# Both feed-forward matrices by Strassen's algorithm, in groups of four token tiles

## The chip, the cores and the metric

The kernel runs on one core of a Trainium2 chip, as one launch. The core has TensorE (PE, matrix products into PSUM; its weight loads are listed as PEld), VectorE (DVE), ScalarE (ACT), GpSimd (POOL) and SyncE (SP, which here only issues DMAs). Each works through its own list of instructions in order, and waits on semaphores for the others. The metric is device time of the whole launch in microseconds.

## The reference, cut to what matters

All data are float32. `x` has 8 batches of 1024 tokens with 512 features: 64 token tiles of 128.

```python
xn = layernorm(x)                                   # over the 512 features
# attention branch, head size 128
local  = softmax(q k^T / sqrt(128)) v               # local_qkv_w
sparse = softmax(only scores >= the 102nd largest of the row) v   # sparse_qkv_w
mem    = concat(p, softmax(p bank^T) bank) @ mem_out_w + b        # p = xn @ memory_proj_w
pred   = gelu((xn @ pred_in_w + b) @ pred1_w + b) @ pred2_w + b
s = concat(local, sparse, mem, pred) @ warboss_w + warboss_b
# feed-forward branch
g = silu(relu(xn @ w1 + b1) @ w2 + b2)              # w1: 512 x 2048, w2: 2048 x 512
out = x + s * g
```

## The kernel before, in words

Tokens are taken per batch (8 tiles), in pairs of tiles (`T` = 256 tokens) for the projections, heads and feed-forward. Normalized tokens are transposed on TensorE into `xnT` (features on partitions), in tiles of four token tiles. Keys, values and queries come from resident weights `w_qkv`; each token tile then has a local and a sparse score row of 1024. The sparse head finds the 102nd largest score on VectorE with 13 rounds of MAX8 and MATCH_REPLACE8 (`sparse_select`). Probabilities are transposed on TensorE, and `attend` multiplies them by the values per pair.

The feed-forward branch goes by pairs. `up` (lines 412 to 433) computes two of the 16 blocks of 128 hidden columns directly: per block four matmuls (128x128 weights by 256 tokens) accumulate over the four 128-row parts of `w1`, which lies in SBUF whole (lines 211 to 214). ScalarE applies bias and Relu from PSUM; GpSimd makes four sums of the 128x128 quarters (lines 427 to 433). `down` (435 to 451) multiplies by `w2` with Strassen's algorithm in its Winograd form: seven products in place of eight per chunk, accumulated over the eight chunks (`NWC`) of a pair in four PSUM banks (`ps_f`). The sums of `w2`'s quarters are made once, written to DRAM, and loaded per chunk as 896 KB tiles with three buffers (`load_w2`, 352 to 370). `make_gate` (383 to 405) copies the seven sums to SBUF, adds them into four quarters on GpSimd, adds the bias and applies Silu. `finish_pair` (686 to 707) waits for gate and heads, multiplies by `warboss_w`, and GpSimd adds the bias, multiplies by the gate, adds `x` and issues the output DMA.

PSUM has four banks in a ring (`ps_r`) for all products that are copied out at once, and the four of `ps_f`.

The order of the work is written out when the program is built. A planner (lines 108 to 170) keeps a clock per engine, counted in matmul columns. Work around the feed-forward consists of chains (generators), each of which says what it next waits for: a clock time, or facts in the set `done`. `run` advances the first chain that is ready; when none is, it takes the next matmul of the feed-forward branch (`filler`) if `may_fill` allows. Instructions stay in the order in which they are emitted on every engine (`InOrder`). Each token tile starts at `begin + n * STEP` of that clock. Thus feed-forward matmuls fill TensorE wherever attention waits for other engines. A wrong estimate in the planner costs nothing by itself: the chip waits on semaphores alone.

Of the kernel before, what the change touches and what calls it, by code (L numbers as in the profile page):

```python
# [15 lines left out]
P = 128  # L16
# [4 lines left out]
def kernel(  # L21
# [50 lines left out]
    ps_f = ctx.enter_context(tc.tile_pool(name="ps_f", bufs=1, space=PSUM))  # L72
# [36 lines left out]
    SLACK = 400  # L109
    rounds = []  # L110
# [20 lines left out]
    def run(until):  # L131

        while not until():
# [8 lines left out]
            else:  # L142
                columns = next(filler, None) if may_fill() else None
                if columns is not None:
                    tick(columns)
                else:
                    times = [c[0] for c in chains if not callable(c[0])]
                    if not times and not rounds and not any(map(is_ready, chains)):
                        raise RuntimeError("nothing is due")
                    tick(max(1, min(times + [clock["pe"] + 200]) - clock["pe"]))  # L150

    def start(generator, due=0):
        chains.append([due, generator])
# [17 lines left out]

    def ring(name, shape):
        return ps_r.tile(list(shape), F32, tag="r", name=name)
# [5 lines left out]
    def load_x(name, b, j):  # L179
        t = sb.tile([P, D], F32, tag="x", name=f"{name}_{b}_{j}", bufs=4)  # L180
        sp.dma_start(out=t, in_=x[b, ts(j, P), :])
        return t


    first_x = [load_x("xl", 0, j) for j in range(4)]
    w_qkv = const.tile([P, ND, 2, 3 * HD], F32, tag="w_qkv", name="w_qkv")
    for h, w in ((SPARSE, sparse_qkv_w), (LOCAL, local_qkv_w)):
        sp.dma_start(out=w_qkv[:, :, h, :], in_=w.rearrange("(c p) n -> p c n", p=P))
        t = sb.tile([P, 2, D], F32, tag="s", name=f"xl_0_{h}", bufs=2)
        for k in range(2):  # L190
            j = len(first_x)
            sp.dma_start(out=t[:, k], in_=x[0, ts(j, P), :])
            first_x.append(t[:, k])

# [16 lines left out]
    w1 = const.tile([P, ND, W], F32, tag="w1", name="w1")  # L211
    w1v = ffn_w1.rearrange("(c p) n -> p c n", p=P)
    for c in range(4):
        pool.dma_start(out=w1[:, :, ts(c, W // 4)], in_=w1v[:, :, ts(c, W // 4)])
    b2 = const.tile([P, D], F32, tag="b2", name="b2")
    pool.dma_start(out=b2, in_=ffn_b2.partition_broadcast(P))
    w_mp = load_const("w_mp", memory_proj_w)
    w_pi = load_const("w_pi", pred_in_w)
    w_p1 = load_const("w_p1", pred1_w)
    w_p2 = load_const("w_p2", pred2_w)  # L220
    w_wb = load_const("w_wb", warboss_w)
# [77 lines left out]
    def project_k(b, g, h):  # L299
        if b not in kT:  # L300
# [4 lines left out]
            [w_qkv[:, c, h, HD : 2 * HD] for c in range(ND)],  # L305
# [6 lines left out]
    def project_v(b, q):  # L312
# [4 lines left out]
        for j in range(2):  # L317
# [3 lines left out]
                [w_qkv[:, c, :, 2 * HD :] for c in range(ND)],  # L321
# [7 lines left out]
    def project_q(b, p):  # L329
        qT[b, p] = sb.tile([P, 2, T], F32, tag="qT", name=f"qT_{b}_{p}", bufs=2)  # L330
        ps = ring(f"pq_{b}_{p}", (P, 2, T))
        for h in range(2):
            accumulate(
                ps[:, h, :], [w_qkv[:, c, h, :HD] for c in range(ND)], pair_xnT(b, p), T
            )
# [7 lines left out]

    H = D // 2
    B11, B21, T2, T3, T4, T1, B22 = range(7)
    w2_dram = [
        dram.tile([P, 7, H], F32, tag=f"w2_{k}", name=f"w2_{k}_dram") for k in range(NWC)
    ]
    w2_tiles = {}
    w2v = ffn_w2.rearrange("(h k p) n -> p k h n", h=2, p=P)  # L350

    def load_w2(n):

        pair, k = divmod(n, NWC)
        if pair >= B * NP:
            return
        w = sb.tile([P, 7, H], F32, tag="w2", name=f"w2_{n}", bufs=3)
        w2_tiles[n] = w
        if pair:
            sp.dma_start(out=w, in_=w2_dram[k])  # L360
            return
        b12 = sb.tile([P, H], F32, tag="tmp", name=f"b12_{k}", bufs=3)
        sp.dma_start(out=w[:, B11 : B21 + 1, :], in_=w2v[:, k, :, :H])
        sp.dma_start(out=w[:, B22, :], in_=w2v[:, k, 1, H:])
        sp.dma_start(out=b12, in_=w2v[:, k, 0, H:])
        pool.tensor_sub(w[:, T1], b12, w[:, B11])
        pool.tensor_sub(w[:, T2], w[:, B22], w[:, T1])
        pool.tensor_sub(w[:, T3], w[:, B22], b12)
        pool.tensor_sub(w[:, T4], w[:, B21], w[:, T2])
        sp.dma_start(out=w2_dram[k], in_=w)  # L370
# [3 lines left out]


    gate = {}
    at_pair = [0, 0]

    def may_fill():
        b, p = at_pair  # L380
        return b == B or needs("constants", ("xnT", b, 2 * p), ("xnT", b, 2 * p + 1))()

    def make_gate(b, p, acc):
        n = f"{b}_{p}"
        m = sb.tile([P, 7, H], F32, tag="m", name=f"m_{n}")
        for c in range(4):
            w = min(2, 7 - 2 * c)
            copy(m[:, 2 * c : 2 * c + w, :], acc[:, 2 * c : 2 * c + w, :], 180 * w)
        add = pool.tensor_add
        add(m[:, 1:3], m[:, 1:3], twice(m[:, 0]))  # L390
        add(m[:, 3:7:3], m[:, 3:7:3], twice(m[:, 2]))
        add(m[:, 6], m[:, 6], m[:, 5])
        add(m[:, 4:6], m[:, 4:6], twice(m[:, 3]))
        g = sb.tile([P, 2, D], F32, tag="g", name=f"g_{n}")
        for j, blocks in enumerate((m[:, 1:7:5], m[:, 4:6])):
            add(
                g[:, j].rearrange("p (h n) -> p h n", h=2), blocks,
                b2.rearrange("p (h n) -> p h n", h=2),
            )
        on("pool", 1200 + 4500)  # L400
        yield after("pool")
        act.activation(g, g, AF.Silu)
        on("act", 700)
        gate[b, p] = g
        done.add(("gate", b, p))

    def feed_forward():

        hidden = {}
        acc = {}  # L410

        def up(b, p, c):
            at_pair[:] = b, p
            ps = ring(f"ph_{b}_{p}_{c}", (P, 2, T))
            h = sb.tile([P, 2, T], F32, tag="h", name=f"h_{b}_{p}_{c}", bufs=3)
            rhs = pair_xnT(b, p)
            for k in range(2):
                w = c + NWC * k
                for d in range(ND):
                    pe.matmul(  # L420
                        ps[:, k, :], w1[:, d, ts(w, P)], rhs[d], start=d == 0, stop=d == ND - 1
                    )
                    yield T
            for k in range(2):
                act.activation(h[:, k, :], ps[:, k, :], AF.Relu, bias=bcol(c + NWC * k))
                on("act", 280)
            a11, a21, a12, a22 = (h[:, k, ts(j, P)] for k in range(2) for j in range(2))
            s = sb.tile([P, 4, P], F32, tag="hs", name=f"hs_{b}_{p}_{c}", bufs=3)
            pool.tensor_add(s[:, 0], a21, a22)
            pool.tensor_sub(s[:, 1], s[:, 0], a11)  # L430
            pool.tensor_sub(s[:, 2], a11, a21)
            pool.tensor_sub(s[:, 3], a12, s[:, 1])
            hidden[b, p, c] = (a11, a12, s[:, 1], s[:, 2], a22, s[:, 0], s[:, 3])

        def down(b, p, c):
            n = (b * NP + p) * NWC + c
            load_w2(n + 2)
            if c == 0:
                acc[b, p] = ps_f.tile([P, 8, H], F32, tag="f", name=f"f_{b}_{p}")
            h = hidden.pop((b, p, c))  # L440
            w = w2_tiles.pop(n)
# [397 lines left out]
```

## Time and profile before

| What | Value |
|---|---|
| Median of 3 runs | 3071.06 us (3070.82 to 3071.55) |
| The profiled execution | 3071.09 us, its span from first to last instruction 3069.0 us |
| Mean granted TensorE clock | 0.997 |
| VectorE, MAX8 on 1024 scores | 832 x 1.23 us |
| GpSimd, 128x128 sums (`hs`) | 1024, about 0.46 us each |
| GpSimd, gate sums (`m`) | 96 of 128x512 at 1.296 us, 32 of 128x256 at 0.754 us |
| ScalarE, Relu out of PSUM (`h`) | 512 of 128x256, 0.471 us |
| ScalarE, copies of gate sums (`m`) | 96 of 128x512 at 0.596 us, 32 of 128x256 at 0.407 us |
| SP, weight chunks from DRAM | 248 loads of 896 KB, 4.6 us to landing |

A row of groups reads: line, engine, operation, output<-inputs by name with buffer numbers left out, shapes, type, count | busy time in total, mean ns of one | idle time before. All instructions have line 85, because one helper issues them; the names tell them apart. `ph` and `f` are the PSUM tiles of the first and second feed-forward product, `h` the hidden units, `hs` the sums of their quarters, `m` the gate's sums, `po` the output product, `pT` the transposed probabilities. TensorE splits a float32 matmul call into two instructions, so its counts are twice those in the code. A chain of waits is followed back from the last instruction, at each step to what released it.

### The profile page before, as it was taken

The page shows a single profiled execution, that of the slowest core. Times are in us where ns is not written, and L with a number is a line of the kernel's source. Part 1 is how long each engine was busy: PE and PEld are TensorE (multiplying, and loading weights), DVE is VectorE, ACT ScalarE, POOL GpSimd, SP SyncE. Part 2 cuts the span into 40 slices and gives each one's busy share as a digit, 9 for nine tenths or more (in the row PEclk, how much of TensorE's full clock was granted, in tenths as well). Part 3 has the DMA queues.
Part 4 walks back from the last instruction along what each step waited for, and adds up shares of the span by engine and source line. Part 5 has one row for each costly group of instructions (what it writes and reads, how often), then busy time and mean ns, then how long its engine had stood idle before and what let it go on. Part 6 is the DMA issues. An engine that isn't in the chain of part 4 may idle for free.

```text
span 3069.0 us, 35608 instructions
## 1 busy us (share of the span) xinstructions
PE 3027.2 (99%) x13380; PEld 2401.8 (78%) x13380; DVE 2290.0 (75%) x3126; ACT 1311.9 (43%) x2321; POOL 1009.5 (33%) x1528
## 2 busy tenths in 40 slices
PE   8999999999999999999999999999999999999997
PEld 6888778887778877888777887877877878778775
DVE  5968768778678777787686785976858868768764
ACT  3444344444444444444443443444444444444443
POOL 3433323332332333323233322333213333133333
PEclk9999999999999999999999999999999999999998
DMA  5433212333123331333313231233312333123321
GB/s 203 156 108 127 102 56 103 108 127 112 57 94 117 112 115 57 108 103 115 105 62 126 91 127 62 100 112 111 114 62 87 118 120 113 55 74 110 110 95 65
DMA packets 76204, 314.69 MB, mean 103 GB/s; under 512 B 8830, under 2 KB 13968, under 8 KB 76032
## 3 DMA queue, kind: packets, MB, share of 16 engines
q1 hardware_dynamic: 68896, 288.91, 27.4%
q0 software_dynamic: 7136, 23.51, 2.0%
q8 instruction: 105, 1.72, 0.2%
q14 instruction: 67, 0.55, 0.1%
HBM read 288.27 MB, written 24.12 MB: 102 GB/s over the span
## 4 chain that ended last, share of the span: by engine, by line
PE 95%; POOL 2%; ACT 1%; DVE 1%; issue 0%; DMA 0%; POOLq 0%; SPq 0%; DVEq 0%
PE ph L85 28%; PE f L85 24%; PE pa L85 7%; PE sc L85 7%; PE po L85 6%; PE pk L85 4%; PE pq L85 4%; PE pv L85 4%; PE ptp L85 4%; PE ppi L85 2%; PE pmp L85 2%; PE pp L85 2%; POOL o L85 1%; PE pmo L85 1%; PE ptx L85 1%; POOL xr L85 1%
## 5 line engine op out<-in xcount | busy, mean ns | idle before, releaser
L85 PE MATMUL ph<-xnT,w 128*128 128x256 f32 x4096 | 965.7, 380 | 0.0
L85 DVE MAX8 top<-left 128x8 f32<-128x1024 f32 x768 | 943.0, 1228 | 26.7
L85 PEld LDWEIGHTS ph<-xnT,w 128*128 128x128 f32 x4096 | 765.4, 190 | 128.4 <-issue 34.7
L85 DVE MATCH_REPLACE8 left<-top,left 128x1024 f32<-128x1024 f32 x704 | 850.7, 1208 | 0.0
L85 POOL TENSOR_TENSOR hs<-h 128x128 f32<-128x128 f32 x512 | 244.9, 478 | 1669.0 <-ACT h L85 1651.3
L85 PE MATMUL f<-w,hs 128*128 128x256 f32 x2048 | 539.5, 379 | 0.0
L85 DVE MAX8 top<-s 128x8 f32<-128x1024 f32 x64 | 78.5, 1227 | 551.4 <-ACT s L85 551.4
L85 PEld LDWEIGHTS f<-w,hs 128*128 128x128 f32 x2048 | 382.7, 190 | 59.4 <-issue 10.7
L85 PE MATMUL f<-w,h 128*128 128x256 f32 x1536 | 420.7, 379 | 0.0
L85 ACT ACTIVATE h<-ph,biasT 128x256 f32<-128x256 f32 x512 | 214.2, 471 | 301.2 <-PE ph L85 300.3
L85 PEld LDWEIGHTS f<-w,h 128*128 128x128 f32 x1536 | 287.4, 190 | 46.0 <-issue 10.4
L85 PE MATMUL sc<-kT,qT 128*128 128x512 f32 x512 | 242.0, 595 | 1.0 <-ACT o L85 0.7
L85 PE MATMUL pa<-pT,v 128*128 128x256 f32 x1024 | 231.3, 379 | 0.0
L85 PE MATMUL po<-w_wb,head 128*128 128x512 f32 x512 | 224.9, 592 | 0.0
L85 PEld LDWEIGHTS pa<-pT,v 128*128 128x128 f32 x1024 | 194.1, 190 | 29.1 <-issue 3.1
L85 ACT COPY pT<-ptp 128x512 f32<-128x512 f32 x256 | 150.1, 589 | 140.0 <-PE ptp L85 137.9
L85 POOL TENSOR_TENSOR m<-m 128x512 f32<-128x512 f32 (+1 forms) x128 | 148.6, 1161 | 151.5 <-ACT m L85 144.0
L85 PEld LDWEIGHTS po<-w_wb,head 128*128 128x128 f32 x512 | 97.3, 190 | 108.8 <-issue 106.7
L85 ACT ACT_TABLE_LOAD x133 | 170.6, 1283 | 16.0 <-DVE nms L85 12.2
L85 PEld LDWEIGHTS sc<-kT,qT 128*128 128x128 f32 x512 | 94.6, 190 | 72.9 <-issue 58.1
L85 ACT COPY el<-sc 128x512 f32<-128x512 f32 x128 | 74.4, 588 | 168.1 <-PE sc L85 167.9
L85 ACT COPY o<-po 128x512 f32<-128x512 f32 x64 | 37.4, 585 | 231.5 <-POOL xr L85 134.2
(111 smaller groups left out, 3246.5 us busy)
## 6 DMA issues: line engine op xcount, KB each, us to landing
w<-w_dram SPq DMA_DIRECT2D x248, 896.0 KB, 4.6
xl<-in_L_attn_x_dram SPq DMA_DIRECT2D x64, 256.0 KB, 4.9
xr<-in_L_attn_x_dram SPq DMA_DIRECT2D x64, 256.0 KB, 5.1
out_dram<-xr POOLq DMA_DIRECT2D x64, 256.0 KB, 2.3
xs<-in_L_attn_x_dram SPq DMA_DIRECT2D x56, 256.0 KB, 4.9
w_dram<-w SPq DMA_DIRECT2D x8, 896.0 KB, 4.6
w<-in_L_ffn_w_dram POOLq DMA_DIRECT2D x4, 1024.0 KB, 14.0
w<-in_L_ffn_w_dram SPq DMA_DIRECT2D x8, 256.0 KB, 5.2
```

What stands on the lines that cost most here:

```text
L85: r = made(*args, **kwargs)
```

## The change

The first product, too, is done by Strassen's algorithm. A group is four token tiles (512 tokens). `w1` is cut into quarters (halves of the 512 features by halves of the 2048 hidden columns, in eight chunks of 128 columns per half), the tokens into quarters too (halves of the features by halves of the 512 tokens). Per group and chunk there are seven products of two matmuls each; before there were 2 x 2 blocks of four matmuls for the same outputs. In detail:

- `token_sums`: four 128x512 sums of token quarters per group on GpSimd, in one buffer `t`.
- Up chunk: seven products through ring banks (two to a bank), copied by ScalarE into `u` (two buffers); four GpSimd additions (`add_products`) combine them into four quarters in place; then ScalarE's Relu with bias, from SBUF (`hidden_units`). The sums for the second product are made by a chain of their own, `hidden_sums`, at most three chunks ahead.
- `plan` writes out the order: an up chunk of group g, then a down chunk of one of its two pairs or of the pair before, and after the last up chunk eight down chunks without an up between.
- `load_chunk`: the sums of `w1` are made once on VectorE (those of `w2` on GpSimd as before), both go to DRAM, and both are loaded per use, three chunks ahead into four buffers. `w1` is no longer resident.
- Small weights: of `w_qkv` only the query part stays resident. Key, value, head-input (`memory_proj_w`, `pred_in_w`) and output (`warboss_w`) weights are loaded into two borrowed buffers (`ws`) at each use, with a count of how many are lent; a chain waits 8000 columns (`AHEAD`) between the load and the use.
- The gate is made in place in `m`; `finish_pair` first joins the heads (output product, bias), and later multiplies by the gate. A down chunk that would refill `m` waits in the planner for `gated` of the pair before. `make_gate` and `finish_pair` come last among ready chains (`rank`), sums first.
- Token tiles `x` have one buffer in place of four, `qT` one in place of two; `xr` and `o` have two. The accumulator is four one-bank tiles in place of one four-bank tile.
- More `needs` conditions state facts that buffers require, and the planner may tick on while nothing is ready.
- `STEP` follows the new matmul count and is 0.98 of it; it was 0.99. `begin` is 1000 columns later.

```diff
-    def load_x(name, b, j):
-        t = sb.tile([P, D], F32, tag="x", name=f"{name}_{b}_{j}", bufs=4)
+    def load_x(name, b, j, tag="x"):
+        t = sb.tile([P, D], F32, tag=tag, name=f"{name}_{b}_{j}", bufs=1 if tag == "x" else 2)
...
+    def can_borrow(n):
+        return lambda: lent[0] + n <= 2
+
+    def borrow(name, *parts):
+        lent[0] += 1
+        t = sb.tile([P, ND, 2 * HD], F32, tag="ws", name=name, bufs=2)
...
+    def on_pool(op, out, in0, in1):
+        getattr(pool, op)(out, in0, in1)
...
+        on("pool", 60 + int(1.42 * n))
...
-    w1 = const.tile([P, ND, W], F32, tag="w1", name="w1")
...
+    def plan():
+        half = NWC // 2
+        for g in range(GROUPS + 1):
+            for k in range(NWC):
+                if g < GROUPS:
+                    yield "up", g, k
+                if k >= half and g < GROUPS:
+                    yield "down", 2 * g, k - half
+                if k < half and g:
+                    yield "down", 2 * g - 1, k + half
+            if g < GROUPS:
+                for n in range(2):
+                    for k in range(half):
+                        yield "down", 2 * g + n, k + half * (1 - n)
...
+        w = sb.tile([P, 7, H], F32, tag="w", name=f"w_{kind}_{n}_{k}", bufs=4)
+        if n:
+            sp.dma_start(out=w, in_=w_dram[kind, k])
+            return
...
+    def add_products(m):
+        for to, add in (
+            (m[:, 1:3], twice(m[:, 0])),
+            (m[:, 3:7:3], twice(m[:, 2])),
+            (m[:, 6], m[:, 5]),
+            (m[:, 4:6], twice(m[:, 3])),
+        ):
+            on_pool("tensor_add", to, to, add)
+            yield
...
+        t = sb.tile([P, 4, 2, T], F32, tag="t", name=f"t_{g}")
+        on_pool("tensor_sub", t[:, 0], b12, b11)
+        on_pool("tensor_sub", t[:, 1], b22, t[:, 0])
+        on_pool("tensor_sub", t[:, 2], b22, b12)
+        on_pool("tensor_sub", t[:, 3], b21, t[:, 1])
+        yield after("pool")
+        tokens[g] = (b11, b21, t[:, 1], t[:, 2], t[:, 3], t[:, 0], b22)
+
+    def hidden_units(g, k, m):
+        for _ in add_products(m):
+            yield pool_is_free
+        yield after("pool")
+        for j, slots in enumerate(((1, 4), (6, 5))):
+            h = sb.tile([P, 2, T], F32, tag=f"h{j}", name=f"h_{2 * g + j}_{k}", bufs=(5, NWC)[j])
+            for u in range(2):
+                act.activation(h[:, u], m[:, slots[u]], AF.Relu, bias=bcol(k + NWC * u))
...
+            if kind == "up":
+                wants[0] = lambda: (
+                    "constants" in done and n in tokens and units_made[0] > n * NWC + k - 2
+                )
+            else:
+                wants[0] = lambda: (n, k) in operands and wanted_at[n, k] <= clock["pe"] and (
+                    k < NWC - 1 or n == 0 or ("gated", *divmod(n - 1, NP)) in done
+                )
...
+            load_chunk(at + 3)
...
+                    for c in range(2):
+                        pe.matmul(
+                            ps[:, i % 2], halves(w[:, i])[:, c], tokens[n][i][:, c],
+                            start=c == 0, stop=c == 1,
+                        )
...
     def finish_pair(b, p):
-        yield needs(("gate", b, p), *[("head", b, p, h) for h in range(4)])
+        yield needs(*[("head", b, p, h) for h in (LOCAL, 2, 3)])
+        if (b, p) != (0, 0):
+            yield needs(("out", *divmod(b * NP + p - 1, NP)))
+        yield can_borrow(2)
+        done.add(("borrowed", b, p))
+        both = [borrow(f"wb_{b}_{p}_{k}", warboss_w[ts(k, T), :]) for k in range(2)]
+        xs = [load_x("xr", b, 2 * p + j, "xr") for j in range(2)]
+        yield clock["pe"] + AHEAD
+        yield needs(("head", b, p, SPARSE))
...
             def two_heads(b=b, p=p):
+                if (b, p) != (0, 0):
+                    yield needs(("borrowed", *divmod(b * NP + p - 1, NP)))
+                yield can_borrow(1)
+                w = borrow(f"wmp_{b}_{p}", memory_proj_w, pred_in_w)
+                yield clock["pe"] + AHEAD
...
-    STEP = int(0.99 * (12400 + NWC * (2 * ND * T + 7 * H) // 2))
+    STEP = int(0.98 * (12415 + NWC * (2 * 7 * T + 2 * 7 * H) // 4))
```

## The prediction

> **What bounds the kernel now.** I read the page first for busy shares, then the chain that ended last, then the waits of TensorE, then pieces of the trace in order of time.
>
> From the page (busy time by engine; SP's DMA queue with packets, MB and share of the 16 DMA engines; the chain by engine; the first group):
>
> ```profile
> PE 3027.2 (99%) x13380; PEld 2401.8 (78%) x13380; DVE 2290.0 (75%) x3126; ACT 1311.9 (43%) x2321; POOL 1009.5 (33%) x1528
> ...
> q1 hardware_dynamic: 68896, 288.91, 27.4%
> ...
> PE 95%; POOL 2%; ACT 1%; DVE 1%; issue 0%; DMA 0%; POOLq 0%; SPq 0%; DVEq 0%
> ...
> L85 PE MATMUL ph<-xnT,w 128*128 128x256 f32 x4096 | 965.7, 380 | 0.0
> ```
>
> TensorE is the bound: 99% busy, 95% of the chain, and the next engine is at 75%. `ph` is the first feed-forward product. It shows 4096 rows for 2048 matmul calls, so one call is two instructions. The means (380 ns) cannot be multiplied out, since ends are modelled and rows overlap. The real price is in the chain in order of time, where a run of matmuls has a length. Its last stretch (start, length, what):
>
> ```profile
> 3031.83 3.45 PE pa L85 x16
> 3035.28 6.49 PE f L85 x30
> 3041.79 1.08 ACT m L85 x2
> ...
> 3047.70 2.45 POOL g L85 x2
> 3050.19 0.94 issue
> 3051.13 0.57 ACT o L85
> ```
>
> 30 instructions of 256 columns take 6.49 us: 216.3 ns each, 432.6 ns a call, 1.69 ns per column of the planner's clock. After `f` ends at 3041.8 no matmul sets the end: gate and output run on ScalarE and GpSimd until 3069.0, 27.2 us.
>
> TensorE's own waits for other engines:
>
> ```profile
> PE ptx L85 <- DVE xl L85: 13.8, 6, 10.0
> PE ptp L85 <- ACT es L85: 3.0, 4, 1.2
> PE ptp L85 <- ACT el L85: 1.0, 2, 0.6
> ```
>
> Only the first 10 us at the start counts. Priced per instruction (216.3 ns for 256 columns, 429 for 512 from `pk` x24 in 10.30 us, 109 for 128), the 13380 instructions stream for about 2997 us. The other 72 us are 27 at the end, some 16 in the first 40 us, and about 29 strewn over 64 token tiles.
>
> **The change, part by part.**
>
> *Matmuls removed.* Before, per pair of tiles, 16 column blocks x 4 depths = 64 calls; 32 pairs give 2048. After, per group of four tiles, 8 chunks x 7 products x 2 halves = 112; 16 groups give 1792. 256 calls go: 256 x 0.4326 = **-110.7 us**, all on the path that sets the end. Shapes stay 128x128 by 128x256, so no price changes. The second product keeps its 1792 calls, and no other matmul is added.
>
> *GpSimd, added sums.* Each up chunk sums its seven products with three 512-wide and one 256-wide add: the `m` adds of the gate have these shapes (1296 and 754 ns by form), so 3 x 1.296 + 0.754 = 4.64 us, x128 = 594 us. Token sums: 4 x 1.296 us x 16 = 83 us. GpSimd goes from 1009.5 to about 1687 us, 57% of the new span. All of it lies beside the matmuls while the planner spaces it: it books 787 columns (1.33 us) for a 512-wide add, near the row, but 241 columns (0.41 us) for a 128-wide one that takes 0.455 plus its gap, with 400 columns (0.68 us) of slack behind a chain. In a stretch without attention work the cover is gone: a group needs 8 x 4.85 + 16 x 1.82 (adds with their gaps) + 5.3 + two gates and outputs (2 x 16.3) = 106 us of GpSimd against 224 x 0.4326 = 97 us of matmul. That costs 9 us per group, and it is met only in the last 50 us or so, by half: 5 us. What is late next would be ScalarE: the Relu that waits for the sums stands in order before copies which free the four ring banks.
>
> *ScalarE, added copies.* Per up chunk three 128x512 copies from PSUM (592 ns) and one of 256 (407): 2.18 us x 128 = 279 us; the 512 Relus stay, now from SBUF. The gate's Silu is cut in two (64 halves, about 4 us). 1312 becomes about 1595 us, 54%. Hidden, but the ring is asked for four banks in 6.06 us of up-matmuls instead of one in 3.46. A bank comes round after three others (some 4 us in pure feed-forward, under 1 us beside transposes, whose bank fills in 0.44 us), and a table load plus exponential on ScalarE is 1.28 + 1.15 us. So some matmuls will wait. The trace has no such ring load; bounds: nothing, and one 1.2 us wait in each of 128 chunks, 150 us. I take **+10 us** with the 5 us above inside it, because the nearest row, all TensorE waits on ScalarE in the old trace, is under 7 us, and POOL and ScalarE stay near half load.
>
> *VectorE.* 32 weight sums for 8 first chunks, about 0.4 us each by my estimate from the 128x512 scalar operation (0.59 us): 13 us on an engine with 25% free. Nothing on the path.
>
> *DMA.* Added: 15 x 8 chunk loads of 0.918 MB = 110 MB, 7 MB written to DRAM once, output weights 32 x 1.05 = 34, head weights 32 x 0.52 = 17, keys and values 16 x 0.52 = 8; residents of 2.6 MB leave SP's queue, w1's 4 MB leave GpSimd's. SP's queue carries about 463 MB; 288.91 MB took 27.4% of 3069 us, 344 GB/s, so 1350 us, 46%. Landing is 4.6 us for a chunk, and three chunks of look-ahead are at least 9 us (three downs alone). Behind a stalled SP wait stand the next chunks: the likeliest is an `xr` load behind the previous pair's output (two GpSimd adds, two issues, 2.3 us landing: some 8 us), inside the 16 us that three chunks take beside attention. Zero, with 5 us of a bad stretch left in the range. The single-buffered `x` tiles make SP wait for VectorE's statistics in the same way; the planner leaves 4000 columns (6.8 us) for them.
>
> *Order and borrowed weights.* A pair's heads and its output share two borrowed buffers (4 KB a partition): 13.5 us (8000 columns) ahead of the heads, 28.3 us for the heads (`ppi` at 96.17 to `pmo` at 124.47 in the chain), 13.5 us ahead of the join, 7 us of `po`, about 3 us of copies: 65 us, against a pair's budget of 2 x 26216 columns = 88.6 us. Hidden. A feed-forward pair's last chunk waits until the pair before is gated, because `m` has one buffer; at least 45 us of matmuls lie between them, against 14 us of gate work. Zero. Accumulator banks are taken over by the next pair directly in half the cases; bank by bank copies leave 2 us. Zero to 10 us, in the range.
>
> *Start.* Tokens, not 6 MB of weights, come first on SP, but filling can start only when token sums (5.3 us of GpSimd) and three chunks of sums are there. Keys and queries cover that until 24 us. Zero, +-5.
>
> *End.* The join of the last pair is done before its gate. After the last `f`: one copy (0.65 us), three adds (3.4; the first runs ahead), two bias adds (2.5), Silu (0.6), four 512-wide operations (5.3), output issue and gaps (1.2) and the 8.1 us that today lie between the last issue and the end: 21.8 against 27.2, **-5.5 us**.
>
> *Sum.* 3069.0 - 110.7 - 5.5 + 10 = 2962.8 us of span. The median of the runs is 2.1 us above the profiled span (3071.06 to 3069.0): **2965 us**.
>
> **Two rules weighed.** The Trainium skill's GPSIMD Engine Reference, Key points, says that GpSimd shares its SBUF interfaces with VectorE and contends with instructions that have two SBUF inputs. The trace shows it (start, length, engine, what):
>
> ```profile
> 720.12 1.28 DVE L85 SCALAR_TENSOR_TENSOR es<-s,top,es 128x1024 f32<-128x1024 f32 x1
> ...
> 720.38 1.33 POOL L85 TENSOR_TENSOR hs<-h 128x128 f32<-128x128 f32 x1 [5.48 <-ACT h L85]
> 721.79 0.46 POOL L85 TENSOR_TENSOR hs<-hs,h 128x128 f32<-128x128 f32 x1
> ```
>
> The add of 0.46 us took 1.33. There are 64 such VectorE instructions: at the worst 64 x 1.28 = 82 us more on GpSimd, 1769 us, 60%. MAX8 and MATCH_REPLACE8, the bulk of VectorE's 2290 us, leave the adds at 0.46 in the neighbouring rows. By the rule carried to all of VectorE's work, GpSimd would have 700 us free for 1687 and the kernel would end near 4000; by the rows it does not bind.
>
> TensorE: Matmul & The Clock Gate, the HAM clock gate, says that an idle window of about 3.4 us halves the clock. The first eight `pk` instructions here take 6.04 us, against 3.43 later, after the idle start; the granted clock's row shows 1.00 there all the same. By it, new stalls count for more only if they reach some 3 us. I expect shorter ones, so the sum stays; if each of 16 group changes stalled once for 4 us and then ran 3.4 us at half rate, it would add 16 x 5.7 = 91 us.
>
> **Rivals.** (1) *Ring and sums hold the matmuls back* (chance 0.2): Relus wait for GpSimd, copies behind them are late, TensorE waits about 0.35 us in each of 128 chunks: 45 us, about 3010. For it: four banks at twice the demand, sums booked short for 128-wide adds. Against: half-loaded engines. (2) *Cleaner than I think* (0.1): none of the 10 us of new waits and half of the 29 strewn us gone: 2941. (3) *Slower by the borrowed buffers* (0.06): heads, join, keys and values queue for two buffers, feed-forward stops at the gate, and the pair's chain sets the pace. It is at 65 us; it decides above 88.6, and the kernel is slower than before above 3071/32 = 96. At 98 us: 3136. Against it: keys and values borrow only seven or eight times; they would have to add 140 us each time. (4) *No net change* (0.02): stalls of just 110 us.
>
> **How the numbers follow.** My forecast, 2965, has 0.62; its own range is 2948 to 2985. Eight in ten: from 2941, where the cleaner case lies, to 3012, which takes in most of rival 1: **2940 to 3012**. Within 0.2% (6 us) is what a measurement here can't tell from no change. Faster 0.92, same 0.02, slower 0.06.
>
> **What would show it.** `ph` at 3584 rows with about the same mean; TensorE still at 98% or more; GpSimd near 1690 us, ScalarE near 1600, DMA near 46%; TensorE's waits on ScalarE under some 20 us in total. Rival 1 shows as TensorE waits `ph <- ACT`, rival 3 as long gaps at batch changes with feed-forward absent. I am wrong if TensorE's busy share falls below 96%, or if matmul prices change with the new sources.

## The result, and the profile after

The changed kernel takes **3025.71 us** (median of 4 runs, 3024.86 to 3028.62) against 3071.07 us: a ratio of 0.9854 (0.9837 to 0.9871). It is faster by 45 us (1.5%, with an interval that excludes no change), where 106 were forecast, and it lies above the range of 2940 to 3012.

From the page of the changed kernel (busy time by engine, SP's DMA queue, the chain by engine, and the two groups of the first product):

```profile
PE 2937.0 (97%) x12868; PEld 2313.2 (77%) x12868; DVE 2334.8 (77%) x3158; ACT 1550.0 (51%) x2864; POOL 1656.3 (55%) x2097
...
q1 hardware_dynamic: 164256, 468.24, 45.6%
...
PE 85%; DVE 5%; ACT 5%; POOL 2%; DMA 2%; issue 1%; SPq 1%; POOLq 0%; DVEq 0%; ACTq 0%
...
L85 PE MATMUL ph<-t,w_up 128*128 128x256 f32 x2048 | 487.6, 380 | 2.7 <-ACT u L85 2.4
...
L85 PE MATMUL ph<-xnT,w_up 128*128 128x256 f32 x1536 | 389.9, 381 | 0.0
```

The work is the forecast work: 512 rows of `ph` fewer (2048 + 1536 = 3584), the same mean of 380 ns, and loads of the other engines within 3% of those foreseen. What differs is the chain: 95% of it was TensorE, now 85%, and VectorE, ScalarE and the DMAs hold 12%.

TensorE's waits, the longest sums of the whole run (us in total, times, longest):

```profile
PE ptx L85 <- DVE xl L85: 12.9, 5, 9.9
PE ptp L85 <- ACT el L85: 9.5, 6, 4.6
PE ptp L85 <- ACT es L85: 7.2, 2, 6.2
PE po L85 <- ACT head L85: 6.3, 1, 6.3
PE f L85 <- ACT m L85: 5.8, 3, 2.2
PE ptm L85 <- DVE em L85: 4.1, 7, 0.9
```

All rows of that view that name ScalarE add up to some 50 us, against 7 before; 29 of the 50 lie in the first 250 us. Single waits of 4.6 to 6.3 us are new, and they lie there too.

**The account that all readings below use.** For each stretch of the span, the instructions that TensorE ran in it are priced as they stream without a gap (429.3, 216.0, 108.7 and 54 ns for 512, 256, 128 and 64 columns, the first three from start to start in these traces, the last half of the third). The stretch less that price is time *lost*. A matmul at a lowered clock counts as lost too. In us, with the edits of the experiments below:

| Kernel | Span | 0–50 | 50–250 | 250–2900 | 2900–end | Lost in all |
|---|---|---|---|---|---|---|
| before | 3069.0 | 16.3 | 1.4 | 29.7 | 21.8 | 71.4 |
| changed | 3023.4 | 18.0 | 38.1 | 58.4 | 20.2 | 136.4 |
| no_build | 2994.9 | 18.4 | 11.7 | 56.9 | 18.9 | 107.9 |
| late_store | 2995.0 | 19.1 | 11.3 | 56.9 | 19.0 | 108.0 |
| no_products | 3016.8 | 20.2 | 29.2 | 58.7 | 19.0 | 129.8 |
| takeover | 2994.0 | 18.2 | 13.9 | 53.4 | 19.3 | 107.0 |
| no_relu | 2991.1 | 19.1 | 12.6 | 50.8 | 19.5 | 104.1 |
| rounds11 | 2989.8 | 19.3 | 13.5 | 48.9 | 19.5 | 102.8 |
| ring3 | 3046.8 | 20.0 | 14.3 | 98.5 | 24.4 | 159.8 |
| before_ring3 | 3094.4 | 16.7 | 2.1 | 53.0 | 22.6 | 96.8 |

(A matmul across a border is priced in both pieces, so the pieces fall up to 3 us short of the whole. staged, relu_split, ahead, first_order, waits and step_099 are told in their own places.)

The price fell by about 111 us, as forecast. The lost time rose by 65: 38 in the first 250 us, 29 strewn over the next 2650, less 2 at the end. These are two questions.

**The first 250 us.** SP's queue in time order in the changed kernel (start, length of the issue, output<-input). `w_up` loads of three and one of `x_up` are the raw quarters of one chunk, `w_up_dram<-w_up` stores a chunk's finished sums:

```profile
23.30 0.34 SPq L85 DMA_DIRECT2D w_up_dram<-w_up  x1
23.68 2.31 SPq L85 DMA_DIRECT2D w_up<-in_L_ffn_w_dram  x3
26.04 0.57 SPq L85 DMA_DIRECT2D x_up<-in_L_ffn_w_dram  x1
31.09 0.34 SPq L85 DMA_DIRECT2D w_up_dram<-w_up  x1
31.47 2.32 SPq L85 DMA_DIRECT2D w_up<-in_L_ffn_w_dram  x3
...
40.53 0.34 SPq L85 DMA_DIRECT2D w_up_dram<-w_up  x1
40.91 2.36 SPq L85 DMA_DIRECT2D w_up<-in_L_ffn_w_dram  x3
...
48.27 0.34 SPq L85 DMA_DIRECT2D w_up_dram<-w_up  x1
```

The next chunk's loads are issued only after the store of the one before, and that store waits for VectorE's sums, which wait for their own raw data. Load, land, add, store: one chunk in 7.7 to 9.4 us, though three are meant to be ahead. (Chunks of `w2`, later in the stretch, wait in the same way for GpSimd's sums.) The chain of waits at one such place, in order of time:

```profile
52.88 4.57 DMA x_up<-in_L_ffn_w_dram
...
57.57 1.44 DVE w_up L85
...
60.33 0.75 DVE w_up L85 x2
61.07 0.09 DVE r_l L85
...
61.18 1.16 ACT el L85
...
62.38 1.11 PE ptp L85 x4
```

TensorE waits for a transpose of probabilities, these for ScalarE's exponential `el`, that for a row's factor `r_l` on VectorE, and `r_l` stands in VectorE's order behind four weight sums whose data landed at 57.45. An attention result is late because of a weight load that it has nothing to do with.

**The other 2650 us** have no such stretch: the page's forty slices show TensorE at nine tenths all the way.

### The profile page after: what moved, and what is told of

Read it like the earlier page. It is cut to its first block, busy times and chain, and to the rows that moved or that the text cites. A ratio compares the mean times of both kernels' runs of the same rounds, so it can differ in the third digit from the quotient of the medians.

```text
span 3023.4 us, 36222 instructions
## 1 busy us (share of the span) xinstructions
PE 2937.0 (97%) x12868; PEld 2313.2 (77%) x12868; DVE 2334.8 (77%) x3158; ACT 1550.0 (51%) x2864; POOL 1656.3 (55%) x2097
## 3 DMA queue, kind: packets, MB, share of 16 engines
q1 hardware_dynamic: 164256, 468.24, 45.6%
## 4 chain that ended last, share of the span: by engine, by line
PE 85%; DVE 5%; ACT 5%; POOL 2%; DMA 2%; issue 1%; SPq 1%; POOLq 0%; DVEq 0%; ACTq 0%
PE f L85 22%; PE ph L85 21%; PE pa L85 7%; PE po L85 7%; PE sc L85 6%; PE pk L85 4%; PE pv L85 4%; PE ptp L85 3%; PE pq L85 3%; DVE top L85 2%; DVE left L85 2%; PE ppi L85 2%; PE pmp L85 2%; PE pp L85 2%; ACT L85 1%; PE pmo L85 1%
## 5 line engine op out<-in xcount | busy, mean ns | idle before, releaser
L85 POOL TENSOR_TENSOR u<-u 128x512 f32<-128x512 f32 (+1 forms) x512 | 591.7, 1157 | 688.8 <-ACT u L85 669.0
L85 PE MATMUL f<-w_down,hs 128*128 128x256 f32 x2048 | 542.0, 381 | 2.5 <-ACT m L85 2.2
L85 PE MATMUL ph<-t,w_up 128*128 128x256 f32 x2048 | 487.6, 380 | 2.7 <-ACT u L85 2.4
L85 PEld LDWEIGHTS f<-w_down,hs 128*128 128x128 f32 x2048 | 383.1, 191 | 70.6 <-issue 21.1
L85 PEld LDWEIGHTS ph<-t,w_up 128*128 128x128 f32 x2048 | 383.4, 190 | 66.1 <-issue 15.5
L85 PE MATMUL f<-w_down,h 128*128 128x256 f32 x1536 | 425.3, 382 | 3.6 <-ACT m L85 3.6
L85 PE MATMUL ph<-xnT,w_up 128*128 128x256 f32 x1536 | 389.9, 381 | 0.0
L85 ACT COPY u<-ph 128x512 f32<-128x512 f32 (+1 forms) x512 | 264.0, 530 | 167.2 <-PE ph L85 165.8
L85 PEld LDWEIGHTS f<-w_down,h 128*128 128x128 f32 x1536 | 287.6, 191 | 57.2 <-issue 18.1
L85 PEld LDWEIGHTS ph<-xnT,w_up 128*128 128x128 f32 x1536 | 287.4, 191 | 49.7 <-issue 14.7
```

Of the source, the lines that this page charges most:

```text
L85: r = made(*args, **kwargs)
```

## The experiments

The theory for the start was the order on SP's queue: the store ahead of the next loads. Its rivals: the build costs this in any order (too many loads, VectorE's order), or GpSimd's additions slow VectorE down. For the strewn loss the candidates were the load of GpSimd, of ScalarE, of VectorE, the hand-over of the accumulator banks, the order of single chains, and the ring of four banks.

**no_build: the sums of the weights are not made** (one load of the same size in their place, so wrong weights; the store stays).

```diff
-            for slot, u, h in ((0, 0, 0), (1, 0, 1), (4, 1, 1)):
-                sp.dma_start(out=halves(w[:, slot]), in_=w1v[:, h, :, u, k])
-            sp.dma_start(out=halves(extra), in_=w1v[:, 0, :, 1, k])
-            on_dve("tensor_add", w[:, 5], extra, w[:, 4])
...
+        sp.dma_start(out=w.rearrange("p s n -> p (s n)"), in_=src[:P, : 7 * H])
```

> The changed kernel, but a chunk's first use loads one block of 896 KB straight from the weight matrices: the four pieces per chunk and the four sums per chunk are left out (so the weights are not Strassen's sums), the store to DRAM stays. The order of the other engines is kept. Theory A (building the 16 weight chunks inside the first group holds TensorE back: 55 us of the first 250 us are not streamed, 16 before the change): the loss in the first 250 us falls from 55 to 15-25 us, the time from 3026 to about 2990. Theory B (the first group loses its time to the order of the work itself, filled by tokens and attention that are not there yet): no more than 8 us are won. What is lost between 250 and 2950 us (57 us, 27 before) stays within 5 us under both.

Measured: 3000.13 us (2996.65 to 3002.37), ratio 0.9768 (0.9754 to 0.9783). By the medians 25.6 us come back; of the 28.5 that the two profiled executions differ by, 26.4 lie between 50 and 250 us. So the build is the start's main cost. The run is a yardstick for a better order of it, not a strict floor, since its store still waits for a landing ahead of the next load.

**late_store: the same work, the store of a chunk issued after the next chunk's raw loads.**

```diff
+            store_built()
             on_dve("tensor_add", w[:, 5], extra, w[:, 4])
...
-        sp.dma_start(out=w_dram[kind, k], in_=w)
+        built.append((kind, k, w))
```

> The changed kernel, computing the same: in the first group the store of a chunk's sums to DRAM is issued on SP after the next chunk's four raw loads instead of before them. Theory A1 (SP stands in order behind the store, which waits for the sums, so the next raw pieces start too late, and VectorE and GpSimd then wait for them): the loss in the first 250 us falls from 55 to about 25-30 us, the time to about 2998. Theory A2 (the sums themselves stand in VectorE's list ahead of selection and row maxima while their data is still in flight; when SP issues matters little): 5-12 us won. Theory B: nothing won.

Measured: 3000.52 us (2996.75 to 3001.7), ratio 0.9768 (0.9754 to 0.9783): as much as leaving the build out. SP's queue in late_store:

```profile
12.36 3.28 SPq L85 DMA_DIRECT2D w_up<-in_L_ffn_w_dram  x3
...
24.04 0.34 SPq L85 DMA_DIRECT2D w_up_dram<-w_up  x1
24.42 2.34 SPq L85 DMA_DIRECT2D w_up<-in_L_ffn_w_dram  x3
...
27.48 0.42 SPq L85 DMA_DIRECT2D w_up_dram<-w_up  x1
```

These two stores lie 3.4 us apart, not 8. What SP's queue waited for in the first 250 us (us in total, times, longest), in the changed kernel and then in late_store:

```profile
SPq L85 <- PE ph L85: 42.1, 5, 16.0
...
SPq L85 <- POOL w_down L85: 27.5, 8, 3.8
...
SPq L85 <- DVE w_up L85: 18.1, 6, 5.6
```

```profile
SPq L85 <- PE ph L85: 89.1, 11, 17.0
...
SPq L85 <- POOL w_down L85: 9.0, 2, 6.8
SPq L85 <- DVE w_up L85: 7.1, 2, 6.8
```

The waits of the stores for sums fall from 45.6 to 16.1 us; SP waits for TensorE to free a buffer instead. VectorE's wait for raw data in the first 260 us, in the changed kernel and then in late_store:

```profile
DVE w_up L85 <- DMA x_up<-in_L_ffn_w_dram: 34.6, 7, 10.0
```

```profile
DVE w_up L85 <- DMA x_up<-in_L_ffn_w_dram: 10.8, 3, 4.7
```

And the stretch from 50 to 250 us (length; busy us and instructions of PE, PEld, DVE, ACT, POOL; granted clock; DMA share; GB/s), changed and then late_store:

```profile
50.00:250.00 200.00, 174.56 (x745) 140.03 (x744) 161.75 (x222) 91.50 (x171) 114.10 (x151) 0.94 0.51 165
```

```profile
50.00:250.00 200.00, 193.11 (x868) 156.87 (x867) 179.85 (x251) 102.85 (x196) 125.17 (x166) 0.99 0.55 192
```

123 more matmul instructions in the same time, with *more* DMA traffic. The granted clock tells the other part of the cost: at 0.94, 6% of 200 us, at most some 12 of the 38 lost, is not waiting but matmuls at a lower clock (at most, because TensorE also stood idle for part of that time).

**staged: the sums, too, one chunk later**, so that no engine should wait for a landing.

```diff
+        store_built()
+        build_sums()
+        raw.append((kind, k, w, extra))
```

> The changed kernel, computing the same: building a chunk is spread over three chunks: its raw loads are issued, its sums are emitted one chunk later, when the data should be there, and its store another chunk's loads later. Theories A1 and A2 together: the loss in the first 250 us falls from 55 to about 20-25 us, about 2993 us. If A1 is the whole of it, no better than the late store alone; if A2 is, most of the gain comes here and not there. Theory B: nothing won.

Measured: 3001.77 us (3000.1 to 3004.3), 0.9775 (0.9761 to 0.979). Nothing beyond late_store. The order on the one queue was all that these three edits could remove.

**no_products: GpSimd's four additions per up chunk left out**, the planner's booking kept.

```diff
-        for _ in add_products(m):
+        for columns in (787, 787, 423, 787):
+            on("pool", columns)
             yield pool_is_free
```

> The changed kernel without the four GpSimd additions per up chunk that combine the seven products (512 instructions, about 592 us of GpSimd); the Relus take raw products instead. The planner still books their time, so the order of all other instructions is kept. Theory C (Relus wait on ScalarE for late GpSimd sums, and the copies that free the ring stand behind them): ScalarE's 44 us of waits on the sums vanish, and the loss between 250 and 2950 us falls from 57 to about 35; 20-30 us won in all. Theory D (ScalarE itself: bursts of copies, four Relus in a row, table loads in front of what TensorE needs, whoever made the sums): 0-8 us won outside the first 250 us.

Measured: 3017.18 us (3015.51 to 3018.59), 0.9823 (0.9807 to 0.9839). Its page:

```profile
PE 2934.2 (97%) x12868; PEld 2310.7 (77%) x12868; DVE 2313.0 (77%) x3158; ACT 1549.8 (51%) x2864; POOL 1068.1 (35%) x1585
```

GpSimd has 588 us less to do, and the strewn loss stays at 58.7 us. By the medians 8.5 us are gained; of the 6.6 between the profiled executions, all lie before 250 us (49.4 lost there against 56.1), where the sums of the weights are made. So GpSimd's additions bear on the start as well, though far less than the order of the store. The largest piece of added work is innocent of the strewn loss.

**takeover: on late_store, a pair's first down chunk also waits in the planner until the pair before is copied out** of the accumulator banks.

```diff
+                    k or freed[0] <= clock["pe"]
...
+                    freed[0] = after("act")
```

> The kernel with the late store (3000.5 us), computing the same; the planner holds the first down chunk of a pair until ScalarE's booked copies of the pair before are done, so that other work comes between. Theory E (accumulator banks taken over at once by the next pair make TensorE wait for the copies of m): the three waits f <- ACT m of together 6 us between 250 and 2900 us vanish, the time falls by 4-8 us. Rival: other waits come in their place, less than 2 us.

Measured: 2996.15 us (2995.51 to 2996.73), 0.9756 (0.9741 to 0.977). By the medians 4.4 us less than late_store, in overlapping intervals; in the trace the waits `f <- ACT m` (three, 5.8 us) are gone, and the strewn loss fell by 3.5. But 1.7 us came back in the first 250 us, and the two profiled spans differ by only 1.0. By its median it is the fastest kernel here that computes the whole reference (1% below the changed one, 2.4% below the one before), with first_order and waits within 1 us of it.

**no_relu: on late_store, the 512 Relus moved to GpSimd as plain copies** (bias and Relu are left out).

```diff
-                act.activation(h[:, u], m[:, slots[u]], AF.Relu, bias=bcol(k + NWC * u))
+                pool.tensor_copy(h[:, u], m[:, slots[u]])
```

> The kernel with the late store, but bias and Relu are left out: GpSimd copies the four quarters of a chunk to the hidden units at the same place in the order, and ScalarE is spared 512 instructions of 0.5 us, 256 us. GpSimd's load rises to some 1800-1900 us. Theory D (ScalarE's load and order cause the new strewn stalls): what is not streamed between 250 and 2900 us falls from 58 us to 35-42, the time by 15-23 us. If many separate causes make it (buffers, heads, accumulators), by less than 8 us; if GpSimd's load mattered after all, the time rises.

Measured: 2991.05 us (2989.33 to 2992.82), 0.9739 (0.9725 to 0.9754). ScalarE falls from 1550 to 1360 us, GpSimd rises to 1838, and the strewn loss goes from 56.9 to 50.8. A small part hangs on ScalarE's load.

**relu_split and ahead: on late_store, a pause of 600 columns between the four Relus of a chunk; and borrowed weights loaded 4000 columns ahead, not 8000 (tokens 2000, not 4000).**

```diff
+                if (j, u) != (1, 1):
+                    yield clock["pe"] + 600
```

```diff
-    AHEAD = 8000
+    AHEAD = 4000
```

> The kernel with the late store, computing the same; the four Relus of a chunk, 1.7 us in a row on ScalarE, are emitted one by one, 600 columns (1 us) apart. Theory D in its form of bursts (copies that TensorE waits for stand behind four Relus): 5-12 us faster. If ScalarE's load as such or other causes make the stalls: within 3 us.

> The kernel with the late store, computing the same; borrowed weights are loaded 4000 columns (6.8 us) ahead of their use in place of 8000, tokens 2000 ahead in place of 4000. Theory F (at the end the last pair's heads and join come after the last feed-forward matmul because the chain of loads is long: po runs from 2998 to 3005 us in the changed kernel): the join moves ahead of the last f, 4-7 us won at the end. Rival: loads that have not landed (4.6 to 6.2 us) stop the engines in order, up to 10 us lost.

Measured: 3011.54 us (3009.66 to 3014.71; 0.9809, 0.9793 to 0.9826) and 3012.44 us (3011.61 to 3014.87; 0.981, 0.9795 to 0.9825). Both are 11 to 12 us *slower* than late_store.

In relu_split the strewn loss even fell by 3 us (53.6); the time went in the first 250 us, 45.3 lost against 30.4. There the transposes of the sparse head wait 10.6 us once for `es`. The chain at that place:

```profile
171.38 6.69 DMA xs<-in_L_attn_x_dram
...
186.87 1.05 ACT es L85
...
187.97 1.97 PE ptp L85 x8
```

A token load `xs` holds VectorE for 6.7 us at the head of its list; the selection behind it ends late, and `es` with it. On SP's queue that load stood behind the last store of the build, which waited 7.1 us for GpSimd's sums (no raw loads come after it, so late_store leaves it in front). It is the fault of the start over again, and says nothing of bursts of Relus.

In `ahead` the strewn loss rises to 69.9. `AHEAD` sets the lead of token loads too (half of it, so 2000 columns), and these are what came late: VectorE waits 47.2 us for `xl` data between 250 and 2900 us, in eleven waits, and TensorE's `ptx <- DVE xl` stands at 19.2 us in ten waits against 13.7 in five. What the shorter lead of the borrowed weights alone costs was not measured. The join did not move ahead of the last `f` either: `po` stands bare for 6.9 us as before, with 18.5 us lost at the end against 19.0.

Both edits change only when the planner emits work. A wrong estimate there does not harm the result, but through the order it costs time.

**first_order, waits, step_099: the order in which chains are emitted.** On takeover, first_order puts the statistics of tiles 4 to 7 behind the transposes of tiles 0 to 3. On that, waits holds local and sparse scores and the memory head back until the planner's ScalarE or VectorE is done. On that, step_099 spaces the tiles by 0.99 of the matmul count, as before the change.

```diff
+        normal(0)
...
+            if g == 0:
+                normal(1)
```

```diff
+        yield after("act", 0)
...
-        on("dve", 300)
-        yield after("dve")
+        on("dve", 600)
+        yield after("dve", 1000)
```

```diff
-    STEP = int(0.98 * (12415 + NWC * (2 * 7 * T + 2 * 7 * H) // 4))
+    STEP = int(0.99 * (12415 + NWC * (2 * 7 * T + 2 * 7 * H) // 4))
```

> The kernel with the late store and held accumulators (2996.2 us), computing the same; the statistics of the second four tokens tiles are emitted behind the transposes of the first four, so that ScalarE's square root for them no longer stands ahead of the first xnT copies. Theory G (ScalarE waits in order up to 8 us for statistics at the start, and pk waits 3.5 us for xnT): the first 50 us lose 15-16 us instead of 18-19, the time falls by 2-4 us. Rival: the later start of the second transposes takes it back, within 1 us.

> As first_order, computing the same; scores follow their queries only after ScalarE's booked work (the single query buffer makes them wait for its copy at once, five waits sc <- qT of together 4 us), and the memory head's softmax is booked 300 columns longer on VectorE with 600 columns more slack (five waits ptm <- em, 4-5 us). Theory H (the strewn stalls are many separate ones, each with its own buffer): these two vanish from TensorE's waits, 4-8 us won. Rival: the order moves and as many others come, within 3 us.

> As waits, with STEP at 0.99 of the matmul count instead of 0.98, as it was before the change. If the pace of token tiles matters (feed-forward falls behind by 2% and then stands alone at the end, or chains crowd each other): 3-8 us either way, visible in the last 100 us or in the strewn stalls. If TensorE's load alone sets the time: within 3 us.

Measured: 2996.81 us (2995.14 to 3002.37; 0.9758, 0.9743 to 0.9772), 2997.15 us (2992.35 to 2999.18; 0.9754, 0.9739 to 0.9768) and 2999.27 us (2997.75 to 3005.07; 0.9769, 0.9752 to 0.9785): no gain in any. The first 50 us did improve by 2.6 (18.2 to 15.6 lost), and 50 to 250 gave it back (13.9 to 16.5). `waits` removed the waits that it aimed at, and the strewn loss still rose from 53.3 to 60.9, as matmuls of other chains now waited. step_099 lost only 22.2 us in the first 250, near the 17.7 of the kernel before, but 68.0 strewn. No single name in the list of waits carries the loss.

**ring3 and before_ring3: one bank less in the ring**, in takeover and in the kernel before. The order of instructions is unchanged.

```diff
-    ps_r = ctx.enter_context(tc.tile_pool(name="ps_r", bufs=4, space=PSUM))
+    ps_r = ctx.enter_context(tc.tile_pool(name="ps_r", bufs=3, space=PSUM))
```

> The kernel with the late store and held accumulators (2996.2 us), computing the same in the same order, with three PSUM banks in the ring instead of four. Theory I (the ring's banks, asked for four times per up chunk, make the strewn stalls): with one bank less they grow steeply, 60 us or more lost. Theory J (the stalls come from results that are late, not from banks): under 15 us.

> The kernel before the change, computing the same in the same order, with three PSUM banks in the ring instead of four. It asks for one bank per up block where the changed kernel asks for four. Theory I: less than 10 us slower, so that the ring tells the two kernels apart. Theory J: about as much slower as the changed kernel is by the same edit.

Measured: 3047.92 us (3046.29 to 3048.74; 0.9923, 0.9906 to 0.9939), 52 above takeover; and 3093.35 us (3093.1 to 3096.35; 1.0074, 1.0059 to 1.009), 22 above the kernel before. TensorE's waits from 250 to 2900 us that name `u`, the longest in takeover and then those in ring3:

```profile
PE pmp L85 <- ACT u L85: 2.9, 3, 1.3
```

```profile
PE ptp L85 <- ACT u L85: 5.6, 5, 1.6
...
PE pp L85 <- ACT u L85: 3.8, 2, 2.1
...
PE pmp L85 <- ACT u L85: 3.0, 3, 1.8
...
PE pms L85 <- ACT u L85: 2.2, 1, 2.2
```

With three banks attention's matmuls wait for the copies `u` of an up chunk; these four rows are 14.6 of the 45 us by which the strewn loss rose, the rest is spread over other names and small gaps. The changed kernel leans on the ring more than twice as hard as the old one; neither theory had the pair of numbers. That is not proof that four banks are what costs it 24 us: with four, the waits that name `u` come to some 3 us in that view. A fifth bank, which would tell, wasn't tried.

**rounds11: on takeover, two of the 13 rounds of the selection left out** (so the threshold is not the 102nd largest).

```diff
+            if r >= ROUNDS - 2:
+                yield ROUND
+                continue
```

> The kernel with the late store and held accumulators, with 10 of the 12 rounds after the first in each selection (it keeps the 86 largest scores instead of 102); the planner still books all, so that the order stays. VectorE is spared some 312 us, a tenth of the time. Theory K (VectorE in order behind its selection delivers row maxima, reciprocals, tokens and small sums of the heads late, and ScalarE's copies and TensorE wait in its wake): what is not streamed between 250 and 2900 us falls from 55 to 30-40 us, the time by 15-25 us. Otherwise: by less than 6 us.

Measured: 2988.75 us (2987.16 to 2991.54), 0.9733 (0.9718 to 0.9747): 7.4 below takeover for 324 us less of VectorE, the strewn loss 48.9 against 53.4. As with ScalarE: something, not the whole.

**What the strewn loss is.** Starts of successive matmuls between 250 and 2900 us, less the streamed price, sorted by what ended the gap (gaps of 0.15 us and more; worked out from both traces): late results of ScalarE for attention and hidden units grew from 7.2 us in the kernel before to 15.5 in late_store; accumulator banks (`f <- ACT m`) from 0 to 6.3; `ptm <- DVE em` from 0 to 4.8; `sc <- ACT qT` (one query buffer in place of two) from 0 to 4.0; `xl` stayed near 4.3; gaps too small to name went from 18.4 to 21.5. Together they make 26 of the 27 us. The list is shown; that each item is a separate cause is argued. Only the accumulator's was removed singly; `em` and `qT` were removed together in `waits`, and others came in their place. A second query buffer wasn't tried, and neither was the added DMA traffic (99 GB/s between 250 and 2900 us before, 160 after) with all else kept, so the cause of most of this loss stays open.

## Why the prediction was wrong, point by point

- **Matmuls removed, -110.7: right.** 512 rows fewer at an unchanged price; the account shows about 111 us.
- **Start, "Zero, +-5": wrong, and the largest miss.** It was +38 us (17.7 to 56.1 lost before 250 us). I costed the three chunks that must be there at the first filling, and called a weight sum "nothing on the path" because VectorE has 25% free. Thirteen more chunks are built while attention runs. I did weigh what stands behind a stalled SP wait, but only for `xr` loads; the wait that counted is the store's, with the next chunk's loads behind it, then VectorE's sums behind those, then attention's small VectorE work. Reordering that one store takes 25 us away and brings the kernel to 3000.5 us, inside the range, though 35 above the forecast. The remaining 12.7 us of the start (30.4 lost in late_store against 17.7) stay open; they are there without the build, too. By TensorE's waits they are `pk <- ACT xnT` (4.2 us, 0.7 before), and `ptp` and `ptm` waiting for `el`, `em` and `es` (6.3 together, 0.4 before).
- **Ring, sums and ScalarE, "+10 us": right in kind, too small.** The strewn loss grew by 28.7. Rival 1 named a time near the measured one (3010), but that is chance: its sign is missing, `ph <- ACT u` is 2.4 us in all, and without the additions the strewn loss stays; most of the miss was at the start. The strewn waits lie in attention, where ScalarE's results come later. My bound, TensorE's waits on ScalarE below 20 us, was passed (some 50; 31 in late_store).
- **The 5 us of a GpSimd-bound tail, inside the +10: not there.** `f` waits for `hs` 0.3 us in the whole run.
- **Accumulator banks, "Zero to 10": 6 us** of waits; without them the strewn loss was 3.5 us less.
- **End, -5.5: was -1.6.** I had the last pair's join done before its gate. The chain at the end (start, length, what):

```profile
2985.90 1.06 PE pmo L85 x4
2986.96 11.42 PE f L85 x52
2998.38 6.88 PE po L85 x16
```

The heads end at 2986.9. The join's `wb` loads went out at 2985.4, behind the last chunk's load on SP's queue, and the planner puts some 13.5 us between load and use; so `f` runs out at 2998.4, and `po` stands bare for 6.9 us. I had added up this very chain (13.5 us before the join, 7 of `po`) as hidden against a pair's budget, and not held it against the end, where no budget is left.
- **Clock: "I expect shorter ones, so the sum stays": wrong at the start**, where waits of 3.2 to 6.3 us came and up to 12 us went to the clock. Nor is some 3 us a safe limit: a wait of 2.3 us was enough once (below).
- **GpSimd 1687, ScalarE 1595, DMA 46%: right** (1656, 1550, 45.6%), and GpSimd did not bind. TensorE at 97% lies between the 98 and the 96 that I had named.
- **Borrowed buffers (rival 3): not seen** as a pace. `ahead` does not test it alone, since it shortens the lead of the tokens too.

By terms, the span was missed by 60.6 us: about 38 at the start, 19 strewn, 4 at the end.

## What to carry to other kernels

A queue that issues in order turns a store that waits for an engine into a wait for every load behind it: cost a build by load, landing, sum and store of each piece in turn, and issue the store after the next loads. An engine's free share says nothing about a late instruction at the head of its list; ask for every added instruction what it waits for and what stands behind it. When many chains share one matmul engine, an edit that cuts one wait can make another: relu_split, ahead, first_order and waits gained nothing here or lost, while takeover and less load on ScalarE or VectorE gave a few microseconds each by the medians. Judge such an edit by a table of stretches: relu_split's loss lay in a part of the run at which it was not aimed.

## What the runs showed of the hardware

**The clock follows stalls, in rows and in prices.** From 50 to 250 us the granted clock was 0.94, and 0.99 once the stalls were gone. One place in mid-run, where TensorE waits for ScalarE 0.21, 1.02 and 2.27 us with two short pieces of work between, and then runs sixteen `pa` (start, length, wait before), in the changed kernel and at the same place in late_store:

```profile
2506.34 6.46 PE L85 MATMUL pa<-pT,v 128*128 128x256 f32 x16 [2.27 <-ACT el L85]
```

```profile
2480.70 3.72 PE L85 MATMUL pa<-pT,v 128*128 128x256 f32 x16 [2.28 <-ACT el L85]
```

The clock's row of the changed kernel from 2500 to 2550 us:

```profile
2500.00:2550.00 50.00, 46.49 (x208) 37.76 (x208) 40.09 (x53) 29.60 (x58) 24.88 (x29) 0.93 0.35 117
```

7% of 50 us is 3.5 us; `pa` took 2.7 us longer than in late_store, where the clock's row shows 1.00 from 2474 to 2500. So after the same waits the clock was halved in one run and not in the other. The longer waits of the changed kernel after the first 50 us (3.2, 4.6, 6.2 and 6.3 us) were each followed by a granted clock of 0.50. The Trainium skill, TensorE: Matmul & The Clock Gate, the HAM clock gate, has an idle window of about 3.4 us halve the clock. The halving agrees; the length does not hold as a limit here, since waits of 2.3 us (above) and 2.8 us (late_store, at 58.72, then 0.50 from 59.05 to 62.47) were enough.

**VectorE beside GpSimd.** A weight sum of 128x256 took 0.42 us in the median, and up to 1.49 (1.44 at 57.57 in the chain above; what stretched these is not shown). The operation `es` with two SBUF inputs, 64 times, as a group before, changed, and with GpSimd's additions left out:

```profile
L85 DVE SCALAR_TENSOR_TENSOR es<-s,top,es 128x1024 f32<-128x1024 f32 x64 | 87.5, 1368 | 4.5
```

```profile
L85 DVE SCALAR_TENSOR_TENSOR es<-s,top,es 128x1024 f32<-128x1024 f32 x64 | 98.1, 1533 | 5.4 <-ACT u L85 0.5
```

```profile
L85 DVE SCALAR_TENSOR_TENSOR es<-s,top,es 128x1024 f32<-128x1024 f32 x64 | 90.2, 1410 | 5.3 <-ACT u L85 0.5
```

1368, 1533 and back to 1410 ns with GpSimd busy for 33, 55 and 35% of the span: GpSimd's additions lengthen VectorE's work. I had weighed only the other direction. In the whole it is small: no_products shortens VectorE's work by 22 us (2334.8 to 2313.0) and the strewn loss by nothing.
